# Image 0 of the symmetric attention with eight transposed runs instead of seven, and the schedule marks moved with them

## The chip, the cores and the metric

The kernel runs on one core of one Trainium2 chip. The metric is the device time of one launch in microseconds; three launches of the kernel before gave 2438.45, 2439.52 and 2439.89 us, and the profiled execution is a fourth one with a time of its own.

The core has five engines with a queue each: TensorE (PE in the profile; PEld is the loading of its weights), VectorE (DVE), ScalarE (ACT), GpSimd (POOL), and SyncE (SP), which here only issues transfers.

## The reference

Four layers run over four images of 64 x 64 pixels and 64 channels, in fp32:

```python
x = _L0_conv_ref(x, ...)   # attention over 4096 pixels: out = softmax(q k^T)^T v ; gamma*out + x
x = _L1_conv_ref(x, ...)   # layer norm, 64->256, 3x3 depthwise, gate, ->64 ; layer norm, MLP
x = _L2_conv_ref(x)        # attention of x with itself, see below
x = _L3_conv_ref(x, ...)   # attention over 4096 pixels with 32 channels, then batch norm
```

The change is in the third of these. It views the array as 64 rows of 4096 numbers per image, so that the scores are taken between entries of the second axis:

```python
B, C, H, W = x.shape
xf = x.reshape(B, C, H * W)
scores = jnp.einsum('bci,bcj->bij', xf, xf)
attn = jax.nn.softmax(scores, axis=-1)
out = jnp.einsum('bcj,bij->bci', xf, attn).reshape(B, C, H, W)
return out + x
```

`scores` is a 4096 x 4096 matrix for each image and it is symmetric: entry (i, j) equals entry (j, i). Its exponentials are therefore symmetric as well (a fixed shift is subtracted in place of the row's maximum), and only the division by the row's sum breaks the symmetry; the kernel divides at the end. The kernel uses this: a block of exponentials can serve twice, once as it is and once transposed.

## The kernel before, in words

The images go through the layers one after another, and two layers are always at work together. An image's layer 1 (vector work: stencils and norms) is cut into small pieces by Python generators and laid in between the pieces of the attention that runs at the time. Around the change it is image 0's symmetric attention (`layer2(0)`) that runs on TensorE, and layer 1 of image 3 (`layer1(3)`) that is laid in between. After it come the symmetric attention of image 1 and then layer 3 of image 0.

**Blocks and steps.** `layer2` cuts the 4096 x 4096 matrix into 8 x 8 blocks of 512 x 512. A pair (h, g) names the output columns h and the summed columns g. One block takes two *steps* (u = 0, 1). A step does this:

- `score`: four matmuls on the four 64 x 64 quarters of the array give a 128 x 1024 tile of scores in PSUM (line 1391; the profile shows eight records, since each fp32 matmul has two);
- two exponentials on ACT write it to an `e` tile in SBUF and leave row sums in `m.zs` (line 1396);
- `products`: four matmuls, again eight records, accumulate `x` times the `e` tile into the output of h (line 1453). They are issued two or three steps behind the scores.

**Transposed runs.** Block (g, h) is the transpose of block (h, g). In the list `PART` (image 0) or `FULL` (images 1 to 3) an integer g is a block used only as it is, and a pair in brackets is a *run*: two blocks, four steps, which are also used transposed, so that blocks (g, h) need not be computed at all. For each step of a run DVE transposes the `e` tile in 32 x 32 pieces into one of two `turned` tiles (line 1409). Three steps after the run's last one, `turned_products` issues 64 matmuls (128 records, line 1479) that read the run's `turned` tile and four rotated copies of `x` in the tile `xr`, and DVE adds the result into the output tile `A` (lines 1492 and 1494). Two of PSUM's three score slots are taken until that addition.

**Column sums.** A transposed block also needs its sums over the other axis. For image 0's group h = 0 POOL adds up the `e` tiles of the runs' steps (line 1432). For the groups h > 0 POOL instead issues one accumulating transfer of 512 KB for each step (line 1426), alternately into the two halves of an `esum` tile; a transfer waits until the one before it into the same half has landed. One more transfer adds the halves (line 1430), and POOL adds two quarters (line 1434). `spread_sums` later reduces the result on DVE (lines 1442 and 1443); it is issued nine steps after the group's last run step.

**Buffers.** The `e` tiles come from six buffers; two steps share one. `xr`, the `esum` tiles and the `own` tiles (copies of PSUM results, line 1465) take from the same six.

**Order.** The queues of PE, ACT, DVE and POOL hold their instructions in the order in which the Python code emits them. SP's queue is ordered by the compiler. The main loop calls item after item; every step of `layer2(0)` is an item, and each one advances two clocks, `conv` (layer 1 of image 3) and `misc`. A generator's piece is emitted when its clock has reached the time that its last `yield` named. In `layer2(0)` a step moves `conv` by 3.3, and by 1.5 in the seven steps around the end of one run, which `slow` names. In `layer2(1)` an item moves it by 3.2. `misc` moves by 1.8 a step and carries `features2(1)`, which transposes image 1's `x` into the keys `ko` (lines 1310, 1313, and transfers at line 1314); it is started at item `f + 88` of the 100 steps, f being the first.

**Layer 1 of image 3 beside it.** By the steps of `layer2(0)` in the kernel before: the first norm is at steps 3 to 12, the stencils (line 1241) run until about step 76, the second pointwise stage (line 1270) is at steps 80 to 83, the second norm (lines 1165 to 1192) from step 84 on, and the last pointwise stages (lines 1206, 1291, 1295) begin at step 99 and reach into image 1's symmetric attention.

Of the kernel before, what the change touches and what calls it, by code (L numbers as in the profile page):

```python
# [691 lines left out]
def fast_path(ctx: ExitStack, tc: tile.TileContext, a: dict, out: bass.AP, bad):  # L692
# [43 lines left out]
    def piece():  # L736
        if turn_of["banks"]:
            return PS[:, bass.ts(new_bank(), 512)]
        return new_ps()[:, 0:512]
# [14 lines left out]
    def new_big(name):  # L754
        return big.tile([128, 4096], F32, tag="big", name=name)
# [236 lines left out]
    def at(i, fn):  # L992
        due.setdefault(i, []).append(fn)
# [309 lines left out]
    def features2(b):  # L1303
        x = X[:, b]
        im[b].ko = ko = new_big("ko")
        kv = ko[:, 0:N].rearrange("p (a e n) -> p a e n", e=2, n=128)
        for g in range(4):
            ps = piece()
            for i in range(4):
                nc.tensor.transpose(ps[:, bass.ts(i, 128)], x[:, bass.ts(4 * g + i, 128)], ident)  # L1310
            for e, copy in enumerate((nc.vector.tensor_copy, nc.scalar.copy)):
                own, other = slice(64 * e, 64 * e + 64), slice(64 - 64 * e, 128 - 64 * e)
                copy(kv[own, bass.ts(g, 4), e, :], ps[own, :].rearrange("p (a n) -> p a n", n=128))
                nc.sync.dma_start(out=kv[other, bass.ts(g, 4), e, :], in_=kv[own, bass.ts(g, 4), e, :])
            yield 3.7
# [1 line left out]
    SIDES = [[(7, (h + 1) % 7), ((h + 2) % 7, (h + 3) % 7)] for h in range(7)]  # L1317
    FULL = [(7, [7])] + [(h, [h] + SIDES[h]) for h in range(6)] + [(6, SIDES[6] + [6])]
    PART = [
        (0, [0, 7, (1, 2), 5, (3, 4), 6]), (1, [1, 2, (5, 6), 3, 4, 7]), (2, [2, 1, 3, 4, 7]),  # L1320
        (3, [3, 1, 2, 4, 7]), (4, [4, 1, 2, 3, 7]), (7, [7, 0, 1, 2, 3, 4]),
        (6, [6, (2, 3), 0, (4, 7), 5]), (5, [5, (2, 3), (4, 7), 0, 6]),
    ]

    def layer2(b, when_free=None):
# [5 lines left out]
        steps, runs = [], []  # L1331
# [12 lines left out]
        begin = [mine[h][0] for h in range(8)]  # L1344
        spread_at = {mine_t[h][-1] + (5 if b else 9): h for h in m.mirrored}
        late_start = 4 if b else 6
        slow = range(runs[2][2] - 3, runs[2][2] + 4)
        used, todo, seen = {}, [], set()
        st = {"e": {}, "T": {}, "esum": {}}

# [185 lines left out]
    def close2(b):  # L1536
        x, m = X[:, b], im[b]
        ps, tot, n = piece(), sums2[:, b, :], 4 * max(m.mirrored) + 4
        cs = m.cs.rearrange("p (j k) -> p j k", k=4)
        for k in range(4):  # L1540
            mm(ps[32 * k : 32 * k + 32, 0:n], sel4, cs[:, 0:n, k], start=True, stop=True)
        g = 0
        while g < 8:
            k = g
            while k < 8 and m.count[k] == m.count[g]:
                k += 1
            nc.vector.tensor_reduce(
                tot[:, 4 * g : 4 * k],
                m.zs[:, m.first[g] : m.first[g] + 4 * m.count[g] * (k - g)]
                .rearrange("p (t k) -> p t k", k=m.count[g]), AX.X, ALU.add,  # L1550
            )
            g = k
        nc.vector.tensor_add(tot[:, 0:n], ps[:, 0:n], tot[:, 0:n])
        rz = sm.tile([128, 32], F32, tag="rz2", name="rz2")
        nc.vector.reciprocal(rz, tot)
        yield
        for i in range(4):
            ps = new_ps()
            for j in range(8):
                c = 1024 * i + 128 * j  # L1560
                nc.tensor.transpose(ps[:, bass.ts(j, 128)], m.A[:, c : c + 128], ident)  # L1561
            blocks_ = ps.rearrange("p (j n) -> p j n", n=128)
            nc.vector.tensor_mul(
                blocks_, blocks_, rz[:, bass.ts(i, 8)].unsqueeze(2).to_broadcast([128, 8, 128])
            )
            xs = x[:, bass.ts(i, 512)].rearrange("p (j h) -> p j h", h=H)
            for o in range(2):
                nc.vector.tensor_add(xs, ps.rearrange("p (j o h) -> p j o h", j=8, o=2)[:, :, o, :], xs)  # L1568
            yield
# [9 lines left out]
    def open3(b):  # L1579
        x, m = X[:, b], im[b]  # L1580
        m.tg = new_big("tg")
        m.th = m.tg[:, 0:1024]
        m.gx = m.tg[:, 1024:2048].rearrange("p (t d) -> p t d", d=32)
        for nb in range(2):
            ps = piece()
            for jj in range(2):
                for s in range(2):
                    k = 2 * s + jj
                    mm(
                        ps[32 * k : 32 * k + 32, :], thw[64 * s : 64 * s + 64, :],  # L1590
                        tok(x, s, 2 * nb + jj), start=True, stop=True,
                    )
            nc.vector.tensor_scalar_add(m.th[:, bass.ts(nb, 512)], ps, V("L3_conv_theta_b"))
            yield 3.0

        m.own = own = m.tg[:, 2048:3072].rearrange("p (s n) -> p s n", s=2)
        for s in range(2):
            ps = piece()
            for j in range(4):
                mm(  # L1600
                    ps[32 * j : 32 * j + 32, :], phw[64 * s : 64 * s + 64, :],
                    tok(x, s, j), start=True, stop=True,
                )
            nc.vector.tensor_scalar_add(own[:, s, :], ps, V("L3_conv_phi_b"))
            yield 3.0
        for i in range(2):
            ps = piece()
            for t in range(8):
                mm(ps[:, bass.ts(t, 64)], x[:, bass.ts(8 * i + t, 128)], gw, start=True, stop=True)
            for s in range(2):  # L1610
                nc.vector.tensor_add(
                    m.gx[:, 16 * s + 8 * i : 16 * s + 8 * i + 8, :],
                    ps.rearrange("p (t s d) -> p t s d", s=2, d=32)[:, :, s, :],
                    gb.unsqueeze(1).to_broadcast([128, 8, 32]),
                )
            yield 3.0

    def keys3(b):
        m = im[b]
        m.ph = new_big("ph")  # L1620
        keys = m.ph.rearrange("p (s n) -> p s n", s=2)
        for j in range(4):
            for k in range(4):
                nc.sync.dma_start(
                    out=keys[32 * k : 32 * k + 32, :, bass.ts(j, 512)],
                    in_=m.own[32 * j : 32 * j + 32, :, :],
                )
# [185 lines left out]
    conv_from, misc_from, misc_to = {}, {}, {}  # L1813
# [9 lines left out]
    for b in range(B):  # L1823
        misc_to[len(items)] = True
        f = len(items)
        if b == 0:
            layer2(b)
            misc_from[f + 88] = [features2(b + 1)]
        else:
            layer2(b, lambda b=b: keys3(b - 1))  # L1830
            turns = close2(b - 1)
            for i in (9 if b == 1 else 8, 11, 21, 31, 41):
                at(f + i, lambda turns=turns: next(turns))
            misc_from[f + 46] = [open3(b - 1)]
            f = len(items)
            misc_to[f] = True
            layer3(b - 1)
            if b + 1 < B:
                turns = features2(b + 1)
                for i in (4, 7, 10, 13):  # L1840
                    between3[f + i] = 2, lambda turns=turns: next(turns)
    f = len(items)
# [174 lines left out]
@with_exitstack  # L2017
def conv_seq_kernel(ctx: ExitStack, tc: tile.TileContext, a: dict, out: bass.AP):
    nc = tc.nc
    flag = ctx.enter_context(tc.tile_pool(name="flag", bufs=1))  # L2020
    bad = flag.tile([1, 1], mybir.dt.int32, name="bad")
    fast_path(tc, a, out, bad)
    n_bad = nc.values_load(bad[0:1, 0:1], min_val=0, max_val=1 << 20)
    with tc.If(n_bad > 0):
        general_path(tc, a, out)
# [37 lines left out]
```

## Time and profile before

| | us |
|---|---|
| median of three launches | 2439.52 (2438.45 to 2439.89) |
| the profiled execution, its own time | 2438.81 |
| its span, first to last instruction | 2437.0 |
| first score of image 0's symmetric attention | 1014.57 |
| first score of image 1's symmetric attention | 1246.44 |
| start of score steps 10, 16, 62, 74 and 86 of image 0 | 1041.00, 1058.88, 1149.93, 1171.03, 1200.58 |

So the part that changes, `layer2(0)`, takes 231.87 us of the span. All times below are counted from the span's start. In a line of groups the columns are: line, engine and operation, tiles and shapes, how many, then busy time, the mean duration of one in ns, and the engine's idle time ahead of them with what ended it. A line of the timeline has its start, the length of the merged piece, engine, line and operation, tiles, and how many instructions are merged; matmuls overlap, so a piece's length is longer than the distance to the next.

### The profile page before, as it was taken

What the parts mean: (1) busy time and instruction counts of PE and PEld (TensorE: products, weight loads), DVE (VectorE), ACT (ScalarE), POOL (GpSimd) and SP (SyncE); (2) the same over time, 40 slices, a digit from 0 to 9 for tenths busy, and PEclk for the clock granted to TensorE, in tenths of its full rate; (3) what the DMA queues carried; (4) which work ended last, traced back from release to release, by engine and by line L of the source; (5) the groups of instructions that cost most, each with busy time, mean ns of one, the idle gap of its engine ahead of it and who ended that gap; (6) DMA issues with size and microseconds to landing.
All of it is one profiled execution on the core that took longest, in us unless ns stands there. A gap on an engine that the chain in (4) does not pass through costs nothing.

```text
span 2437.0 us, 63657 instructions
## 1 busy us (share of the span) xinstructions
PE 2408.3 (99%) x27509; PEld 914.1 (38%) x27509; DVE 1461.6 (60%) x1787; ACT 1643.0 (67%) x3140; POOL 553.5 (23%) x395
## 2 busy tenths in 40 slices
PE   9999999999999999999999999999999999999998
PEld 3343453336433543343344442144421344421113
DVE  2020278227832774278667668876668766678886
ACT  4656766666666666668655459954479744579996
POOL 2000000000000000030136562256632365622220
PEclk9999999999999999999999999999999999999999
DMA  3000000010000000030540028710076400386665
GB/s 80 1 18 1 19 1 19 18 19 1 19 18 6 14 19 18 20 77 2 113 97 20 20 65 155 156 28 23 16 153 136 96 21 21 76 169 140 136 136 134
DMA packets 68390, 139.03 MB, mean 57 GB/s; under 512 B 13084, under 2 KB 34309, under 8 KB 68101
## 3 DMA queue, kind: packets, MB, share of 16 engines
q0 software_dynamic: 25040, 89.17, 18.3%
q1 hardware_dynamic: 42309, 43.85, 8.0%
q8 instruction: 218, 3.57, 0.6%
q10 hardware_dynamic: 752, 1.85, 0.2%
q14 instruction: 71, 0.58, 0.1%
HBM read 4.80 MB, written 4.19 MB: 4 GB/s over the span
## 4 chain that ended last, share of the span: by engine, by line
PE 90%; DVE 4%; ACT 4%; issue 1%; DMA 0%; SPq 0%; ACTq 0%; DVEq 0%
PE PS L1096 18%; PE PS L1122 18%; PE PS L1391 10%; PE PS L1453 10%; PE PS L1646 9%; PE PS L1707 9%; PE PS L1479 7%; PE PS L1206 2%; ACT e L1657 2%; DVE tg L1698 1%; ACT e L1396 1%; PE PS L1171 1%; PE PS L1270 1%; PE PS L1561 1%; PE PS L1064 1%
## 5 line engine op out<-in xcount | busy, mean ns | idle before, releaser
L1101 ACT ACTIVATE e<-PS 128x1024 f32<-128x1024 f32 x512 | 523.7, 1023 | 337.7 <-PE PS L1096 301.7
L1396 ACT ACTIVATE e<-PS 128x512 f32<-128x512 f32 x632 | 370.9, 595 | 329.7 <-PE PS L1391 310.5
L1096 PE MATMUL PS<-X,q 64*64 64x512 f32 x4096 | 573.6, 590 | 2.6 <-DVE X L979 1.7
L1122 PE MATMUL PS<-e,vq 64*64 64x512 f32 x4096 | 575.8, 592 | 0.0
L1657 ACT ACTIVATE e<-PS 128x512 f32<-128x512 f32 (+2 forms) x588 | 500.1, 920 | 58.3 <-PE PS L1646 37.5
L1698 DVE TENSOR_TENSOR tg<-tg,e 128x2048 f32<-128x2048 f32 x165 | 377.8, 2290 | 51.1 <-ACT e L1657 40.9
L1391 PE MATMUL PS<-ko 64*64 64x512 f32 x2528 | 334.3, 596 | 0.9 <-DVE X L1568 0.5
L1453 PE MATMUL PS<-e,X 64*64 64x512 f32 x2528 | 327.3, 590 | 1.1 <-ACT own L1465 1.1
L1432 POOL TENSOR_TENSOR esum<-esum,e 128x1024 f32<-128x1024 f32 x132 | 314.0, 2379 | 60.2 <-ACT e L1396 52.9
L1241 DVE SCALAR_TENSOR_TENSOR y<-pad,vec,y 128x1024 f32<-128x1024 f32 x240 | 308.9, 1287 | 18.2 <-ACT y L1237 10.9
L1432 POOL TENSOR_TENSOR esum<-e 128x1024 f32<-128x1024 f32 x22 | 52.2, 2371 | 1177.2 <-ACT e L1396 1171.4
L1409 DVE STREAM_TRANSPOSE turned<-e 128x1024 f32<-128x1024 f32 x196 | 240.6, 1238 | 108.5 <-ACT e L1396 108.2
L1646 PE MATMUL PS<-tg,ph 32*64 32x512 f32 x4096 | 294.9, 612 | 1.7 <-ACT e L1657 0.8
L1096 PEld LDWEIGHTS PS<-X,q 64*64 64x64 f32 x4096 | 182.9, 133 | 262.3 <-issue 181.5
L1122 PEld LDWEIGHTS PS<-e,vq 64*64 64x64 f32 x4096 | 183.5, 133 | 253.3 <-issue 156.3
L1707 PE MATMUL PS<-e,tg 128*32 128x512 f32 x2048 | 272.5, 604 | 0.0
L1679 POOL DMA_DIRECT2D xn<-e x130 | 113.3, 898 | 319.5 <-ACT e L1657 225.9
L1109 DVE TENSOR_REDUCE sums<-zs 128x1 f32<-128x4 f32 x128 | 19.7, 154 | 275.0 <-ACT e L1101 274.8
L1453 PEld LDWEIGHTS PS<-e,X 64*64 64x64 f32 x2528 | 97.5, 133 | 174.1 <-issue 154.4
L1391 PEld LDWEIGHTS PS<-ko 64*64 64x64 f32 x2528 | 90.0, 132 | 167.8 <-issue 145.5
L1646 PEld LDWEIGHTS PS<-tg,ph 32*64 32x64 f32 x4096 | 63.3, 129 | 222.7 <-ACT e L1657 190.2
L1396 ACT ACTIVATION_READ_ACCUMULATOR e<-PS 128x1 f32 x632 | 127.2, 201 | 0.0
(219 smaller groups left out, 1681.2 us busy)
## 6 DMA issues: line engine op xcount, KB each, us to landing
xn<-e POOLq DMA_DIRECT2D x146, 512.0 KB, 5.3
esum<-e POOLq DMA_DIRECT2D x20, 512.0 KB, 5.4
xn<-t SPq DMA_DIRECT2D x64, 128.0 KB
ph<-tg SPq DMA_DIRECT2D x64, 128.0 KB
xn<-X SPq DMA_DIRECT2D x224, 32.0 KB
xr<-X SPq DMA_DIRECT2D x176, 32.0 KB
ko<-ko SPq DMA_DIRECT2D x32, 128.0 KB
xr<-in_x_dram SPq DMA_DIRECT2D x13, 256.0 KB
```

What stands on the lines that cost most here:

```text
L1096: mm(ps[64 * c : 64 * c + 64, bass.ts(r, 512)], m.q[rows_, 128 * t + 64 * c : 128 * t + 64 * c + 64], x[rows_, bass.ts(g, 512)], start=Tru ...
L1101: act(es[g // 2][:, bass.ts(g % 2, 1024)], ps, AF.Exp, bias=SHIFT0, accum_out=zs[:, g : g + 1],)
L1122: ins = mm(PS[64 * s : 64 * s + 64, 2048 + 512 * j : 2560 + 512 * j], vq[rows_, :], es[j // 2][rows_, k : k + 512], start=t == 0 and i < 2 ...
L1241: stt(y1, win, wt, y1, ALU.mult, ALU.add)
L1391: mm(ps[64 * c : 64 * c + 64, bass.ts(r, 512)], m.ko[rows_, k : k + 64], m.ko[rows_, bass.ts(h, 512)], start=True, stop=True,)
L1396: act(e[:, bass.ts(r, 512)], ps[:, bass.ts(r, 512)], AF.Exp, bias=SHIFT2, accum_out=slot(g, 2 * u + r),)
L1432: nc.gpsimd.tensor_add(esum, st["e"][mine_t[h][0]] if k == 1 else esum, e)
L1453: mm(st["acc"][r][64 * c : 64 * c + 64, :], xw[rows_, 4 * g + 2 * u + c, :], st["e"][n][rows_, bass.ts(c, 512)], start=n == mine[h][0], st ...
L1646: mm(PS[64 * c : 64 * c + 64, bass.ts(banks[k], 512)], m.ph[32 * k : 32 * k + 32, 128 * mc + 64 * c : 128 * mc + 64 * c + 64], m.th[32 * k ...
L1657: act(e[:, 512 * lo : 512 * k], PS[:, 512 * banks[lo] : 512 * banks[lo] + 512 * (k - lo)], AF.Exp,)
L1698: nc.vector.tensor_add(esum, esum, e)
L1707: mm(st["y"][32 * k : 32 * k + 32, :], m.gx[:, i % 32, :], es[i][:, bass.ts(k, 512)], start=mc == 0, stop=i % 32 == 31,)
```

## The change

Two rows of `PART` are reordered and shortened, and one row is shortened.

- Group h = 0 had the order 0, 7, run (1, 2), 5, run (3, 4), 6. It becomes 0, 5, run (1, 2), run (3, 4), run (6, 7): blocks 6 and 7, computed directly before, are now also used transposed. Its steps 4 to 15 are all run steps.
- Group 7 no longer computes block 0 and group 6 no longer computes block 0, since these are the transposes of the new run. Group 6 becomes 6, 5, run (2, 3), run (4, 7).

In all 96 steps instead of 100, and eight runs instead of seven. The new run takes index 2, so `slow` names run 3 for image 0 (the same run (1, (5, 6)), still ending at step 23), and `features2(1)` starts at item `f + 84`, which is again twelve items before the end.

```diff
     PART = [
-        (0, [0, 7, (1, 2), 5, (3, 4), 6]), (1, [1, 2, (5, 6), 3, 4, 7]), (2, [2, 1, 3, 4, 7]),
-        (3, [3, 1, 2, 4, 7]), (4, [4, 1, 2, 3, 7]), (7, [7, 0, 1, 2, 3, 4]),
-        (6, [6, (2, 3), 0, (4, 7), 5]), (5, [5, (2, 3), (4, 7), 0, 6]),
+        (0, [0, 5, (1, 2), (3, 4), (6, 7)]), (1, [1, 2, (5, 6), 3, 4, 7]), (2, [2, 1, 3, 4, 7]),
+        (3, [3, 1, 2, 4, 7]), (4, [4, 1, 2, 3, 7]), (7, [7, 1, 2, 3, 4]),
+        (6, [6, 5, (2, 3), (4, 7)]), (5, [5, (2, 3), (4, 7), 0, 6]),
     ]
...
-        slow = range(runs[2][2] - 3, runs[2][2] + 4)
+        slow = range(runs[3 if b == 0 else 2][2] - 3, runs[3 if b == 0 else 2][2] + 4)
...
         if b == 0:
             layer2(b)
-            misc_from[f + 88] = [features2(b + 1)]
+            misc_from[f + 84] = [features2(b + 1)]
```

## The prediction, made before the result was known

> **What bounds the kernel now.** I read the page's busy shares and chain first, then its part around image 0 by stretches of time, then TensorE's own timeline there.
>
> ```profile
> PE 2408.3 (99%) x27509; PEld 914.1 (38%) x27509; DVE 1461.6 (60%) x1787; ACT 1643.0 (67%) x3140; POOL 553.5 (23%) x395
> ...
> PE 90%; DVE 4%; ACT 4%; issue 1%; DMA 0%; SPq 0%; ACTq 0%; DVEq 0%
> ```
>
> ```profile
> 1014.50:1043.00 28.50, 27.43 (x240) 8.68 (x240) 10.17 (x14) 17.63 (x49) 7.09 (x3) 1.00 0.33 68
> 1043.00:1070.00 27.00, 26.88 (x440) 12.51 (x437) 18.24 (x20) 18.52 (x49) 11.05 (x5) 1.00 0.05 12
> 1070.00:1171.00 101.00, 99.91 (x1024) 36.54 (x1020) 90.91 (x94) 82.35 (x235) 5.73 (x7) 1.00 0.15 35
> 1171.00:1210.00 39.00, 39.00 (x518) 15.18 (x514) 21.41 (x32) 23.32 (x67) 8.52 (x10) 1.00 0.70 150
> 1210.00:1246.40 36.40, 34.92 (x492) 15.59 (x488) 19.63 (x26) 20.87 (x59) 6.41 (x8) 1.00 0.85 175
> ```
>
> The five lines of the second fence are stretches: length, then busy us of PE, PEld, DVE, ACT, POOL, the granted clock, the DMA share, GB/s. PE is busy nearly throughout, at full clock. DVE is nearly full only while the stencils run (90.91 of 101); before 1070 it idles 27 of 55.5 us. Transfers matter only at the end (0.70 and 0.85). "Busy" alone does not show that PE issues without pauses, so I read distances between starts:
>
> ```profile
> 1058.02 1.04 PE L1453 MATMUL PS<-e,X 64*64 64x512 f32 x8
> 1058.88 1.04 PE L1391 MATMUL PS<-ko 64*64 64x512 f32 x8
> 1059.74 1.04 PE L1453 MATMUL PS<-e,X 64*64 64x512 f32 x8
> 1060.71 3.71 PE L1479 MATMUL PS<-turned,xr 32*64 32x256 f32 x128
> 1064.35 1.09 PE L1391 MATMUL PS<-ko 64*64 64x512 f32 x8
> 1065.26 1.04 PE L1453 MATMUL PS<-e,X 64*64 64x512 f32 x8
> ```
>
> A score group and a product group each follow the last after 0.86 us, however long they look, and most of the 231.87 us has this cadence. Adding up every pause over it between 1010 and 1246 gives only 4.5 us. So this part is bound by the number of matmul groups, and what the change takes away there should show.
>
> [...] here a run starts 0.97 after the group ahead of it and the second group after it lies 0.91 from the first, 0.16 more than the cadence. [...] a 512 KB accumulating transfer takes about 5.5 us at 1184 and 9.3 us (1218.08 to 1227.35) while SP's transfers are under way.
>
> **Removed from PE.** Blocks (7, 0) and (6, 0): 2 blocks x 2 steps x (score + product) = 8 groups x 0.86 = 6.88 us. ACT loses 4 x 2 exponentials with their sum readings, 8 x (0.60 + 0.20) = 6.4 us, off the path.
>
> **Added to PE.** One transposed run. Ahead, 1059.74 to 1065.26 is 5.52 us; without the run these would be two groups, 1.72. So 3.80 us. Net on PE: 6.88 - 3.80 = 3.08, **-3.1 us**.
>
> **Added elsewhere.** DVE: 4 transposes x 1.24 + 4 additions to `A` x 0.415 = 6.6, and 0.69 more in group 7, whose block 7 is no longer fresh in `A`. The 6.6 fall into steps 8 to 19, where DVE idles 27 us; there they cost nothing. Without that cover, among the stencils, DVE has 10 us idle in 101: it would still find room, with the stencils up to 6.6 us later and PE waiting for their pieces by at most that. The third run's product is issued at item 18, three steps after its transposes. POOL: four more additions x 2.37 = 9.5 us, eleven in a row from 1032; with the two later runs PE needs about 33 us for these steps, POOL 26, so it is never far behind. The `turned` tile of run 2 is that of run 0, read at item 10 and rewritten from item 12: no wait.
>
> **SP.** The rotated copies for h = 6 wait for the last turned product of h = 0. That moves from 1064.4 to about 1071, so they are issued at 1071 to 1082 in place of 1064 to 1075, and those for h = 5 shift likewise from 1085. They are needed at about 1188; the next thing behind them on SP begins at 1175 today. Free.
>
> **Layer 1 of image 3.** Steps 0 to 95 move its clock as before, so its pieces stay at the same step numbers. Four lost steps x 3.3 = 13.2 ticks go to image 1's part, 13.2 / 3.2 = 4 items later. Its PE work is the same and PE bounds that part too (52.76 of 53.6 busy, pauses of 1 us). Zero, either way 1 us.
>
> **The end of the part, where steps and side work meet anew.** Steps 74 and on are the same run, 3.8 us later (1174.8). But group 6's second run now follows the first without a break, group 5 starts at 82, its run at 84, and the keys `ko` come at items 84 to 90 instead of 88 to 94, so that the second norm (84 to 88) falls among them. Three things could run late.
>
> ```profile
> 1196.91 0.86 POOL L1426 DMA_DIRECT2D esum<-e  x1 [1.98 <-ACT e L1396]
> 1202.87 0.86 POOL L1430 DMA_DIRECT2D esum<-esum  x1 [5.09 <-DMA esum<-e]
> 1207.97 1.27 POOL L1434 TENSOR_TENSOR esum<-esum 128x512 f32<-128x512 f32 x1 [4.24 <-DMA esum<-esum]
> ...
> 1215.39 0.65 PE L1310 MATMUL PS<-ident,X 128*128 128x128 f32 x4 [0.17 <-ACT ko L1313]
> ...
> 1220.30 0.65 PE L1310 MATMUL PS<-ident,X 128*128 128x128 f32 x4 [0.66 <-ACT ko L1313]
> ...
> 1225.20 0.66 PE L1310 MATMUL PS<-ident,X 128*128 128x128 f32 x4 [0.66 <-ACT ko L1313]
> ```
>
> First, `e` buffers. Eight transfers in two alternating chains from 1178, about 6 us per pair, end near 1202, the final one and POOL's addition near 1209. Only then can group 5's first two transfers go out; landing near 1216. At step 90 all six buffers are taken (`xr`, two `esum`, steps 84 to 89), so its exponential needs those two landed. PE gets there near 1221: 5 us to spare. Second, the pauses at the key transposes: PE waits for a copy on ACT, which waits for one on DVE behind a transpose. Beyond the usual 0.5 us between groups they make 0.25 + 0.74 + 0.74, and the run after them took 4.53 instead of 3.71: 2.5 us today. They may vanish or double, -2.5 to +2.5; the same neighbours recur, so I take 0. Third, the norm's matmuls waited 1.3 us for ACT among run steps at 1027 and wait for nothing at 1201; 0 to +1.3, I take 0.
>
> **Sum.** Against the profiled execution: span 2437.0 - 3.1 = 2433.9; with 1.8 around it, 2435.7 instead of 2438.81. The runs' median lies 0.7 above that execution, so 2439.52 - 3.1 = **2436.4 us**. 0.2% is 4.9 us, about what a measurement of this kernel can tell from no change; the gain is under it.
>
> **Rivals.**
> - *Less waiting as well.* The crowded end loosens: transfers start 4 us earlier and keys 1 and 2 leave before the norm's eight transfers. If the 2.5 us of pauses go, 2433.9. For: SP now sends six of eight key transfers after the norm's. Against: the ACT-behind-DVE chain does not depend on transfers.
> - *Keys late.* SP's order is the compiler's. The norm's eight transfers took 13 us (1214.0 to 1227.0) and six key transfers went behind them, until 1238, eight us before image 1's first score, which needs the last keys. The norm now starts near 1219 and that score comes near 1242; keys behind it would cost up to 3 us: 2439.4.
> - *Slower: the chain of accumulating transfers becomes the bound.* From 1178 to the release for step 90 there are six transfers in a row with 5 us to spare; each may take 0.8 us longer before PE waits. At the 9.3 us seen under load, 3.5 longer, 21 - 5 = 16 us lost: 2452. Against: group 6's chain ran beside 32 of SP's transfers at 5.1 to 6.1 us each, and in the new order has much the same company.
>
> **Chances and range.** As forecast 0.57, less waiting 0.22, keys late 0.12, chain 0.09. The likeliest case's own range is 2434.0 to 2439.0 (the norm, 1 us of layer 1, half of the key pauses). The range of all, 2432.5 to 2441.0, takes in -2.5 with 1 us more, and +2.5 + 1.3 with 0.8 more; it leaves out the chain and some 0.07 at the low end. Faster than 2434.6: 0.20 of the second case and 0.03 of the first, 0.23. Slower than 2444.4: the chain and 0.01 of late keys, 0.10. The rest, 0.67.
>
> **What would show it.** Right: 96 score steps, 8 x 128 records at line 1479; image 1's first score near 1242.5 to 1243.5, since one group of layer 1 also slips behind it; step 62 near 1153.7, 3.8 later than today; step 90 with no wait for POOL's transfers. Wrong: pauses over 1 us among steps 8 to 19 (DVE or POOL late), an exponential at step 90 or later that waits for `esum`, a first score of image 1 that waits for SP, or a difference that appears only after 1300.

## The result

Six launches of the changed kernel gave 2447.46 to 2450.97 us, median 2449.15; six of the kernel before on the same chip 2438.45 to 2439.89, median 2439.14. The ratio is 1.0041, interval 1.0031 to 1.0052: slower by 10.0 us, where 2436.4 was forecast and 2441.0 was the upper end. The profiled execution took 2450.52 us, its span is 2448.7.

The page of the changed kernel first, its busy times and the shares of the chain that ended last:

```profile
PE 2410.6 (98%) x27573; PEld 916.8 (37%) x27573; DVE 1468.4 (60%) x1796; ACT 1639.5 (67%) x3123; POOL 565.5 (23%) x399
...
PE 44%; DVE 6%; ACT 3%; issue 1%; DMA 0%; SPq 0%; ACTq 0%; DVEq 0%; POOL 0%
```

PE has 64 more matmul records, as the change implies (128 for the new run, less 64 for the eight groups that went), and its busy time rose by only 2.3 us. In the chain POOL is new, with 0%, and the shares add up to 54% where they were 99%: followed back from the end, the chain breaks off in the middle of the span. Its earliest pieces in order of time (start, length) are these:

```profile
1095.40 0.15 POOL cs L1440
...
1095.58 0.04 DVE cs L1443
...
1097.80 0.34 DVE A L1492
...
1098.18 1.99 PE PS L1391 x8
```

It ends at a POOL instruction of 0.2 us that waited for no other engine's work. Stretches of image 0's part, in the columns of the kernel before, show the same place:

```profile
1014.90:1043.00 28.10, 27.02 (x232) 8.43 (x224) 12.51 (x16) 17.39 (x49) 10.11 (x5) 1.00 0.32 69
1043.00:1070.00 27.00, 27.00 (x516) 14.60 (x520) 18.85 (x19) 17.58 (x46) 19.71 (x8) 1.00 0.01 3
1070.00:1108.00 38.00, 31.22 (x382) 11.85 (x366) 26.05 (x31) 16.72 (x52) 5.16 (x7) 0.91 0.41 98
```

The third is unlike the others: PE idles 6.8 of 38 us and the clock is 0.91. TensorE's timeline there (start, length, then in brackets the idle time ahead and what ended it):

```profile
1090.22 1.09 PE L1391 MATMUL PS<-ko 64*64 64x512 f32 x8
1091.13 1.04 PE L1453 MATMUL PS<-e,X 64*64 64x512 f32 x8
1098.18 1.99 PE L1391 MATMUL PS<-ko 64*64 64x512 f32 x8 [6.01 <-DVE A L1492]
1099.94 1.93 PE L1453 MATMUL PS<-e,X 64*64 64x512 f32 x8
1101.65 1.93 PE L1391 MATMUL PS<-ko 64*64 64x512 f32 x8
1103.36 1.40 PE L1453 MATMUL PS<-e,X 64*64 64x512 f32 x8
1104.59 1.03 PE L1391 MATMUL PS<-ko 64*64 64x512 f32 x8
```

Step 28's score starts 7.05 us after the group ahead of it instead of 0.86, which is 6.19 lost. The next four groups take 6.41 us (1098.18 to 1104.59) instead of 4 x 0.86 = 3.44: 2.97 more. Together 9.16 us. PE waits for DVE's additions to `A`, which free the score slots of run 3. So VectorE's timeline:

```profile
1085.12 0.70 DVE L1442 STREAM_TRANSPOSE esum<-esum 128x512 f32<-128x512 f32 x1
1095.58 0.69 DVE L1443 TENSOR_REDUCE cs<-esum 128x16 f32<-128x512 f32 x1 [9.76 <-POOL cs L1440]
...
1097.38 0.42 DVE L1494 COPY A<-PS 128x256 f32<-128x256 f32 x1
```

DVE wasn't busy. It stood for 9.76 us at `spread_sums` of group 0, whose reduction waits for POOL's line 1440, and run 3's additions (its matmuls ended at 1090.3) stood behind it. Line 1440 is `nc.gpsimd.memset(m.cs, 0.0)`: the zeroing of the tile that receives all column sums of the image, 0.20 us long, issued inside `spread_sums` when that is called for image 0's first group. POOL's timeline shows why it was late:

```profile
1077.15 0.57 POOL L1426 DMA_DIRECT2D esum<-e  x1 [8.99 <-ACT e L1396]
...
1083.12 0.87 POOL L1426 DMA_DIRECT2D esum<-e  x1 [0.83 <-ACT y L1237]
1089.24 0.86 POOL L1430 DMA_DIRECT2D esum<-esum  x1 [5.25 <-issue]
1094.15 1.26 POOL L1434 TENSOR_TENSOR esum<-esum 128x512 f32<-128x512 f32 x1 [4.04 <-DMA esum<-esum]
1095.35 0.20 POOL L1440 MEMSET cs<- 128x128 f32 x1
```

Line 1426 issues the four accumulating transfers of group 1's run, at steps 20 to 23; the first and the last of them are shown. The next (line 1430) adds the two halves and waits until the last of the four has landed (the line names no releaser, but the trace has that landing at 1088.73, just ahead of 1089.24); the addition waits until that one has landed in turn. The zeroing, which waits for nothing of its own, is queued behind both and starts at 1095.35, as the addition ends (1095.41). The kernel before, same view:

```profile
1076.15 0.90 POOL L1426 DMA_DIRECT2D esum<-e  x1 [1.68 <-DMA esum<-e]
1076.72 0.55 POOL L1440 MEMSET cs<- 128x128 f32 x1
1078.01 0.87 POOL L1426 DMA_DIRECT2D esum<-e  x1 [0.74 <-DMA esum<-e]
```

There it lay between the third and the fourth transfer, and DVE reached its reduction at 1078.90 without a wait. The group's last run step was 13 and is now 15, so the call of `spread_sums`, nine steps behind it, went from item 22 to item 24, while group 1's run stayed at steps 20 to 23: the call, and POOL's instruction in it, was moved past the last two transfers.

That is most of it, not all. I cut the two traces at the first scores of images 0, 1 and 2 and sorted TensorE's time by what each group computes (distance from one start to the next). "Image 1's part" runs from image 1's first score to image 2's; layer 3 of image 0 lies in it.

| distance of starts, after minus before, us | image 0's part | image 1's part |
|---|---|---|
| scores | -2.89 | 0.00 |
| products | +5.69 | +3.31 |
| transposed runs | +4.27 | +0.63 |
| last stages of layer 1 (L1206, L1295) | -0.91 | +0.3 |
| norms of layer 1 (L1171) | -0.18 | |
| all | +5.99 | +4.24 |

The 9.16 us are in image 0's column. But image 1's part, which the change doesn't touch, lost 4.2 us too; of these 0.9 are a group of line 1206 that now falls behind the cut.

### The profile page after: what moved, and what is told of

Its sections match the earlier page's. It is cut to its first block, busy times and chain, and to the rows that moved or that the text cites. A ratio compares the mean times of both kernels' runs of the same rounds, so it can differ in the third digit from the quotient of the medians.

```text
span 2448.7 us, 63782 instructions
## 1 busy us (share of the span) xinstructions
PE 2410.6 (98%) x27573; PEld 916.8 (37%) x27573; DVE 1468.4 (60%) x1796; ACT 1639.5 (67%) x3123; POOL 565.5 (23%) x399
## 4 chain that ended last, share of the span: by engine, by line
PE 44%; DVE 6%; ACT 3%; issue 1%; DMA 0%; SPq 0%; ACTq 0%; DVEq 0%; POOL 0%
PE PS L1646 9%; PE PS L1707 9%; PE PS L1391 8%; PE PS L1453 8%; PE PS L1479 7%; ACT e L1657 2%; DVE y L1241 2%; DVE tg L1698 1%; ACT e L1396 1%; DVE turned L1409 1%; PE PS L1609 1%; PE PS L1561 1%; DVE A L1468 0%; PE PS L1600 0%; PE PS L1206 0%
## 5 line engine op out<-in xcount | busy, mean ns | idle before, releaser
L1432 POOL TENSOR_TENSOR esum<-esum,e 128x1024 f32<-128x1024 f32 x136 | 324.8, 2388 | 62.3 <-ACT e L1396 54.7
```

Source lines behind the costliest of these rows:

```text
L1432: nc.gpsimd.tensor_add(esum, st["e"][mine_t[h][0]] if k == 1 else esum, e)
```

## The experiments

Two theories stand behind most of the expectations. **Theory M**: the zeroing's place in POOL's queue cost some 9 us. **Theory S**: the four lost steps shift the last pieces of layer 1 of image 3 by four items, and where they now lie in image 1's part they cost some 3 us. The rivals for the first are that the third run itself overloads DVE around steps 19 to 28, or that a later reduction costs in proportion to its lateness; for the second, that the loss comes from the new order at the end of image 0's part, the keys above all. Here are all the runs, with both parts from each profiled execution. The ratio is not the quotient of the two medians; the two differ most where the launches of one kernel scatter (e7, e8, e12).

| kernel | median, us | before beside it | ratio and interval | image 0's part | image 1's part |
|---|---|---|---|---|---|
| before | 2439.14 | | | 231.87 | 338.85 |
| after | 2449.15 | 2439.14 | 1.0041, 1.0031 to 1.0052 | 237.86 | 343.09 |
| e1_memset_first | 2440.32 | 2439.07 | 1.0004, 0.9995 to 1.0013 | 229.26 | 343.10 |
| e2_before_spread24 | 2447.24 | 2439.07 | 1.0032, 1.0020 to 1.0045 | 239.86 | 338.86 |
| e3_spread22 | 2440.79 | 2439.07 | 1.0006, 0.9997 to 1.0015 | 229.12 | 343.08 |
| e4_spread23 | 2449.85 | 2439.07 | 1.0043, 1.0026 to 1.0060 | 238.86 | 343.08 |
| e5_before_shift | 2442.28 | 2439.17 | 1.0013, 1.0006 to 1.0020 | 230.83 | 343.46 |
| e6_fix_spread_conv | 2441.58 | 2439.17 | 1.0011, 1.0004 to 1.0017 | 234.29 | 338.88 |
| e7_fix_keys83 | 2443.10 | 2439.17 | 1.0013, 1.0006 to 1.0020 | 231.41 | 343.40 |
| e8_keys82 | 2445.63 | 2439.17 | 1.0022, 1.0012 to 1.0032 | 239.02 | 339.84 |
| e9_fix_early_conv | 2441.75 | 2439.41 | 1.0010, 1.0002 to 1.0018 | 233.41 | 338.88 |
| e10_before_early_conv | 2442.07 | 2439.41 | 1.0012, 1.0005 to 1.0018 | 239.81 | 334.50 |
| e11_fix_early_conv2 | 2446.75 | 2439.41 | 1.0030, 1.0018 to 1.0041 | 239.04 | 338.90 |
| e12_fix_even_conv | 2439.91 | 2439.27 | 1.0008, 1.0000 to 1.0017 | 233.35 | 338.84 |

### The zeroing

**e1: the changed kernel, with the zeroing at step 0.** The allocation of its tile goes with it; nothing else moves.

```diff
+                if b == 0:
+                    m.cs = sm.tile([128, 128], F32, tag="cs2", name="cs2", bufs=1)
+                    nc.gpsimd.memset(m.cs, 0.0)
...
-            if h == m.mirrored[0]:
+            if h == m.mirrored[0] and b:
...
-                if b == 0:
-                    nc.gpsimd.memset(m.cs, 0.0)
```

> The changed kernel, with one edit: the zeroing of cs on POOL is emitted at step 0 of image 0 instead of with the first reduction of column sums at step 24. Theory M (the zeroing, moved in POOL's queue behind the four transfers of group 1, their final transfer and POOL's addition, held DVE for 9.8 us, so PE for 6.6 us and then at half clock): the 9.2 us that steps 27 to 32 took longer than before go away, 2449.2 - 9.2 = 2440.0 (2438.5 to 2441.5), and step 27 to step 28 takes 1.7 to 1.8 us. Theory D (DVE simply has too much to do with four more transposes and copies among the stencils): no change, 2448 to 2450. Theory C (the accumulating transfers of groups 6 and 5 bound the end of the part): no change either.

Measured: 2440.32 us, 8.8 below the changed kernel. The reduction is issued at the same place as after the change and no longer waits (its lines have numbers one to three higher in this kernel); run 3's additions follow as soon as the run lets them:

```profile
1085.21 0.70 DVE L1443 STREAM_TRANSPOSE esum<-esum 128x512 f32<-128x512 f32 x1
1085.95 0.69 DVE L1444 TENSOR_REDUCE cs<-esum 128x16 f32<-128x512 f32 x1
...
1090.60 0.42 DVE L1495 COPY A<-PS 128x256 f32<-128x256 f32 x1 [2.78 <-PE PS L1480]
```

The work is the same, with one 0.2 us instruction elsewhere. Theory M holds and the rival of an overloaded DVE falls. Image 1's part is unchanged at 343.1.

**e2: the kernel before, with group 0's reduction at step 24**, that is, the mark's move alone, without the third run.

```diff
-        spread_at = {mine_t[h][-1] + (5 if b else 9): h for h in m.mirrored}
+        spread_at = {mine_t[h][-1] + (5 if b else 11 if h == 0 else 9): h for h in m.mirrored}
```

> The kernel before, with one edit: the first reduction of column sums (group 0), and the zeroing of cs with it, at step 24 instead of 22; all blocks and runs as before. Theory M: in POOL's queue the zeroing now comes after the addition that ended at 1090.7, DVE waits for it from about 1081, and the copies of run 2, which PE needs for step 28, come some 6 us late; with slow clock after it 6 to 9 us are lost: 2445 to 2448.5. Theories D and C: nothing was added to DVE and nothing changed at the end: 2439.1 within 1.

Measured: 8.2 us slower than before, with the same signature in POOL's, DVE's and PE's timelines:

```profile
1090.51 0.20 POOL L1440 MEMSET cs<- 128x128 f32 x1
```

```profile
1090.74 0.69 DVE L1443 TENSOR_REDUCE cs<-esum 128x16 f32<-128x512 f32 x1 [9.86 <-POOL cs L1440]
```

```profile
1093.34 1.98 PE L1391 MATMUL PS<-ko 64*64 64x512 f32 x8 [6.32 <-DVE A L1494]
```

So the loss needs no third run. Image 1's part is as before to 0.01 us: the 4.2 us there have another cause.

**e3 and e4: the changed kernel, with the reduction at step 22 and at step 23.** If what counts is the number of steps, e4 should lie between e3 and the changed kernel; if it is the place between two transfers, e3 recovers all and e4 nothing.

```diff
-        spread_at = {mine_t[h][-1] + (5 if b else 9): h for h in m.mirrored}
+        spread_at = {mine_t[h][-1] + (5 if b else 7 if h == 0 else 9): h for h in m.mirrored}
```

(e4 has 8 in place of 7.)

> The changed kernel, with the reduction of group 0 and its zeroing at step 22, two steps earlier, where the kernel before had it. Theory M: the zeroing goes out between POOL's transfers of group 1, as before: 2440.0 (2438.5 to 2441.5). Theories D and C: 2448 to 2450.

> The changed kernel, with the reduction of group 0 and its zeroing at step 23, one step earlier. Theory M, by the place in POOL's queue: step 23 is the last of group 1's run, whose last transfer, final transfer and addition are emitted ahead of the reduction in the same step, so the zeroing is as late as at step 24: 2447.5 to 2450.5. If the loss came from the reduction being late in time, in proportion to the steps, this would lie half way, near 2444.5.

Measured: 2440.79 for e3, the same as e1; in it the zeroing goes out at 1081.34 between transfers three and four. e4 took 2449.85, as slow as the changed kernel. There the zeroing comes at 1095.56, and since DVE reaches the reduction a step sooner, it waits a step longer, 10.77 us instead of 9.76. It is a threshold between two neighbours of one queue and not a slope.

### Image 1's part

**e5: the kernel before, with layer 1's clock standing still in the last four steps.** Image 3's pieces reach image 1's part 13.2 ticks behind, as after the change; the rest is the kernel before.

```diff
-                conv.tick(1.5 if n in slow else 3.3)
+                conv.tick(0.0 if n >= 96 else 1.5 if n in slow else 3.3)
```

> The kernel before, with one edit: the last four of the 100 steps of image 0 do not move the clock of layer 1 of image 3, so that its last pieces meet image 1's part four items later, as in the changed kernel; nothing else changes. Theory S (with the zeroing out of the way 3.4 us of the forecast gain are lost because these pieces now meet the closing of image 0 and the transposes of image 1, where PE waits for DVE): 2439.1 + 1.5 to 3.5, so 2440.5 to 2442.5. Rival (the loss has to do with the runs and the keys at the end of image 0, not with these pieces): 2439.1 within 0.7.

Measured: 2442.28, 3.1 us slower, and image 1's part 343.46. The chain of waits settles it. TensorE's waits in image 1's part (what waits, for whom: total us, times, longest), first the changed kernel, then this run, then the kernel before:

```profile
PE PS L1479 <- DVE X L1568: 1.3, 1, 1.3
PE PS L1479 <- DVE u L1291: 0.6, 1, 0.6
PE PS L1206 <- DVE X L1568: 0.5, 1, 0.5
PE PS L1391 <- DMA ko<-ko: 0.3, 1, 0.3
PE PS L1453 <- DVE A L1468: 0.3, 1, 0.3
```

```profile
PE PS L1479 <- DVE X L1568: 1.3, 1, 1.3
PE PS L1479 <- DVE u L1291: 0.6, 1, 0.6
PE PS L1206 <- DVE X L1568: 0.5, 1, 0.5
PE PS L1206 <- ACT e L1396: 0.3, 1, 0.3
PE PS L1453 <- DVE A L1468: 0.3, 1, 0.3
```

```profile
PE PS L1391 <- DVE X L1568: 0.5, 1, 0.5
PE PS L1391 <- DVE u L1291: 0.4, 1, 0.4
```

Four of the waits are the same ones to 0.1 us. Only the wait for the keys' transfers is the changed kernel's own. It is 0.3 us here and 1.2 us in e1, and since it ends with image 1's first score it belongs to image 0's part. Theory S holds, and the keys explain nothing of the 4.2 us in image 1's part.

**e7 and e8: the keys sooner.** e7 is e1 with `features2(1)` one item earlier; e8 is two items earlier, together with the faster clock of e6 below.

```diff
-            misc_from[f + 84] = [features2(b + 1)]
+            misc_from[f + 83] = [features2(b + 1)]
```

> The changed kernel with the zeroing at step 0, and with the keys of image 1 started one item earlier (83). With the zeroing moved, the first score of image 1 waited 1.2 us for the last keys, which SP sent behind the second norm's transfers. If the last two key transfers stay behind the norm's, nothing changes (2440.3); if they come ahead of some of them, the wait goes and 2439.1 is reached.

> Both edits of the run before last (zeroing at step 0, 3.96 in the last 20 steps), and the keys of image 1 started two items earlier (82). If theory S and the wait for the keys add up, 2435.5 to 2437.5, under the kernel before by its 3.1 us or nearly; if the keys' copies at items 82 to 88 hold PE at the denser pieces, as much as the run without this edit or more.

Measured: both slower, 2443.10 and 2445.63, against 2440.32 of e1 and 2441.58 of e6. In e7 the 1.2 us for the keys' transfers are gone, as hoped. But a transposed run waits 1.8 us for the key copy on ACT, and a group of line 1206 waits 1.4 us for the norm on DVE. In e8 a transposed run waits 2.3 us for ACT, and a group of line 1206 waits 2.8 us for DVE's additions at 1246.5. After that last wait the clock stood at 0.50 to 0.51 for 6.00 us (last section). So the wait for the keys can be removed, but starting them earlier cost more than the 1.2 us it gave back.

### Can the shift be undone?

e6, e9, e11 and e12 start from e1 and let layer 1 run faster in image 0's part, so that it reaches image 1's part where it did before: in the last 20 steps, in steps 6 to 19, in steps 8 to 15, and evenly. e10 has e9's edit in the kernel before, as a control. "The first of these three", in the text for e11, is e9.

```diff
-                conv.tick(1.5 if n in slow else 3.3)
+                conv.tick(1.5 if n in slow else 3.96 if n >= 76 else 3.3)           # e6
+                conv.tick(1.5 if n in slow else 4.25 if 6 <= n < 20 else 3.3)       # e9, e10
+                conv.tick(1.5 if n in slow else 4.95 if 8 <= n < 16 else 3.3)       # e11
+                conv.tick(1.5 if n in slow else 3.45)                               # e12
```

> The changed kernel with the zeroing at step 0, and with the clock of layer 1 of image 3 moved by 3.96 instead of 3.3 in each of the last 20 steps of image 0 (13.2 in all, what the four lost steps took away). Theory S: its last pieces meet image 1's part where they did before, most of the 3.4 us come back, 2436.5 to 2438.5. Rival: still 2440.3, or worse where the denser pieces at the end of image 0 hold PE.

> The changed kernel with the zeroing at step 0, and with the clock of layer 1 of image 3 moved by 4.25 instead of 3.3 in steps 6 to 19 of image 0 (13.3 in all, what the four lost steps took away), where DVE idled half of the time. From step 20 on, layer 1 then stands four steps further, so that its second norm and its last pieces meet the end of image 0 and image 1's part as in the kernel before. Theory P (the run itself gains the 3.1 us of the sum, and the rest was lost to the changed company): 2436.0 to 2437.5. Rival (the second run of group 6 right behind the first costs what the sum gains, whatever the company): 2438.5 to 2440.5.

> The kernel before with the same edit of the clock in steps 6 to 19 and nothing else: a control. If the earlier layer 1 is worth something by itself, this is faster than 2439.1 too, by as much as it explains of the run above. Theory P: the pieces at the end now come four steps early and leave image 1's part sooner, so 2437.5 to 2440; no gain of 3 us by itself.

> As the first of these three, with the 13.2 ticks put into steps 8 to 15 alone (4.95 a step). Theory P: the same 2436.0 to 2437.5, unless the first pieces of the stencils now hold PE; then up to 1.5 us more. Rival: 2438.5 to 2440.5.

> The changed kernel with the zeroing of the sums' tile early, and layer 1 of image 3 moved by 3.45 instead of 3.3 in every step outside the slow ones: 89 x 0.15 = 13.35 ticks, which is what the four lost steps took (13.2). The catch-up is spread evenly, where it was put into the first steps or the last ones in the runs before this one and lost there what it won in image 1. Theory S, that the pieces of layer 1 which slip into image 1's part cost about 3 us there and that an even catch-up costs nothing in image 0's part: 2440.3 - 3.1 = 2437.2 us, 2436.0 to 2438.4, with image 1's part back at about 339 us and image 0's part at most 230. Rival, that layer 1 has no slack anywhere in image 0's part: 2440 to 2443, with image 1's part at about 339 us but image 0's part at 231 or more.

Measured: wherever the catch-up was put, image 1's part came back to 338.84 to 338.90, 4.2 us shorter than in e1, and image 0's part grew by nearly the same: 5.0 us in e6, 4.15 in e9, 4.1 in e12. The control e10 shows the same exchange from the other side: 4.35 us won in image 1's part, 7.9 lost in image 0's. e11, with the same catch-up in only eight steps, lost some 6 us against e1. So the times forecast by theories S and P were missed in all five runs; e9 and e11 came out slower than their rival's range as well, and e6 and e12 lie at or near theirs. In e6 and e11 the clock fell in stretches of image 0's part, to a mean of 0.63 over 2.70 us from 1207.30 and to 0.50 over 3.00 us from 1072.30, which makes their losses larger; in e10 the four groups after a wait, from 1070.05 to 1075.23, took 5.18 us instead of 3.44. In e9 the clock was 1.00 around a wait of 2.4 us (1063.00 to 1070.00), and e12's mean over its profiled execution was 0.999. No version beat the kernel before; e12's 2439.91 is 0.64 above it, interval 1.0000 to 1.0017. VectorE and TensorE of e12, at the run that ends at 1046.5, show one such loss:

```profile
1043.42 1.25 DVE L1412 STREAM_TRANSPOSE turned<-e 128x1024 f32<-128x1024 f32 x1 [1.33 <-ACT e L1399]
1044.59 4.48 DVE L1192 TENSOR_TENSOR xn<-xn,X 128x1024 f32<-128x1024 f32 x2
1048.99 1.40 DVE L1495 COPY A<-PS 128x256 f32<-128x256 f32 x4
```

```profile
1046.50 1.09 PE L1394 MATMUL PS<-ko 64*64 64x512 f32 x8
1049.78 1.09 PE L1206 MATMUL PS<-xn,pw 64*64 64x512 f32 x8 [2.20 <-DVE A L1495]
```

DVE idles 1.33 us, then two norm operations of 2.24 us each stand in front of the run's additions, and PE waits for those. On average DVE has room in this stretch; in the order of its queue it hasn't, since every run brings a moment at which PE needs it at once. Later in the same kernel another 2.1 us are lost to such an addition, at 1077.7; the two waits together are 4.3 us, and image 0's part grew by 4.1. The third run isn't needed for such a loss: in e10, which doesn't have it, an addition held PE for 3.2 us at 1070.05.

## Why the prediction was wrong, point by point

- **"Removed from PE" and "Added to PE", net -3.1: right for the matmul groups.** In e1, where the zeroing is out of the way, image 0's part is 2.61 us shorter, of which 0.91 is a group of layer 1 that slipped into image 1's part, as the prediction said. So 1.7 of the 3.1 arrived; new waits, below, took the rest. Scores and products fell by 5.81 (6.88 less some new pauses), transposed runs rose by 4.27: 3.64 for one more run, from its start to the next group's, and 0.63 because slowed runs lost more than before. (The other 0.16 of the forecast 3.80 lies in the groups around the run.)
- **The step that failed: what the change moves.** The prediction went through PE, DVE, POOL and SP for the third run, and through the marks `slow` and `features2`. It didn't look at the third mark that follows the run list, `spread_at`. The description of the kernel gives its rule ("nine steps after the group's last run step") but only the two DVE lines of `spread_sums`, not the zeroing on POOL. With the mark went one POOL instruction past two transfers. "POOL ... is never far behind" counted the additions of group 0, and these indeed ended at 1068.2, before group 1's first transfer at 1077.15. What held POOL was not work but a wait for landings, from 1083.1 on. Measured: +8.8 us by medians (e1), 9.16 by the trace. None of the signs that the prediction lists looks at steps 24 to 28, where it happened.
- **"Layer 1 of image 3. Zero, either way 1 us": wrong.** The argument was that PE bounds image 1's part too, and that the work is the same. Both are true and didn't matter; it is the neighbours that differ. Measured by itself (e5): +3.1 us. The prediction priced three meetings of steps and side work at the end of image 0's part from single waits; this one it dismissed by an average.
- **"They cost nothing" for DVE's 6.6 us in steps 8 to 19: almost.** Steps 8 to 18 kept their cadence. At step 20 the score waited 0.8 us for the additions of run 2, which stood behind two stencils (2.59 us at 1071.09): step 20 is 4.60 us later than before against the start of the part in e1, where 3.80 was forecast. And line 1270 waits 0.7 us for DVE at 1197, which is new.
- **The end of the part: right on balance.** The pauses at the key transposes went, 1.5 us in the list of waits of before, none after; two runs were slowed (4.62 and 4.25 us long instead of 3.71), where before it was one (4.53), and the first score of image 1 waited 0.3 us for its keys, 1.2 in e1. So "less waiting" and "keys late" both happened, and nearly cancelled.
- **The rival "slower", by the chain of accumulating transfers: right sign, wrong place.** Group 6's and group 5's transfers waited for each other, but no exponential of these steps waited for `esum`. What decided was the first such chain, group 1's, near 1083, and through an instruction that has nothing to do with it.
- **The time.** Without the zeroing's loss the changed kernel is at 2440.3 (e1). That lies inside the range given, but by luck: the range was made wide mainly for other losses, at the end of the part. Against the kernel before beside it e1 is 1.25 us slower where 3.1 faster was forecast, so 4.3 us are missing. The shift of layer 1 explains 3.1 of them (e5). Most of the rest lies in image 0's part, which by the trace is 1.4 us longer than forecast. There e1's list of waits has three that are new, 1.2 us for the keys, 0.8 at step 20 and 0.7 at line 1270, and has lost the 1.5 at the key transposes.

Left open: the 0.8 us at step 20 and the 0.7 at line 1270 weren't tried alone, and the keys' 1.2 us were removed only together with a new loss (e7). Whether another rate in image 1's own items would take the shifted pieces without waits wasn't tried either; so what is shown is that the shift costs 3 us and that image 0's part can't absorb it at four rates, not that no schedule can.

## What to carry to other kernels

When an edit moves a call, list every instruction it issues on every engine and, for each, the instructions it is moved past: a 0.2 us memset behind two waits for landings cost 9 us, and sat in no busy time. Give instructions without inputs (a zeroing, an allocation) the earliest place, so that no queue's waits can stand in front of them (8.8 us in e1). And work that is laid in beside a saturated engine isn't free because its engine idles on average: moved by four items it met other neighbours and gave back as much as the shorter loop was to win (3.1 us in e5).

## What the runs showed of the hardware

TensorE's pause in the changed kernel, idle for 6.01 us, cost more than its length. The granted clock after it was 0.50; this is its view by stretches:

```profile
1092.00:1098.00 6.00, 0.17 (x4) 0.00 (x0) 2.42 (x4) 0.63 (x3) 1.40 (x2) 0.94 0.43 94
1098.00:1104.00 6.00, 5.82 (x28) 1.79 (x32) 5.86 (x8) 1.64 (x5) 0.00 (x0) 0.50 0.14 36
1104.00:1108.00 4.00, 4.00 (x40) 1.29 (x36) 2.68 (x3) 2.77 (x11) 0.00 (x0) 0.99 0.00 0
```

Four groups ran at 0.50 and cost 2.97 us beyond the pause. e8 shows the same after a much shorter pause, idle for 2.81 us:

```profile
1246.50:1249.50 3.00, 2.98 (x16) 1.05 (x20) 0.62 (x2) 0.93 (x1) 0.87 (x1) 0.50 0.18 37
1249.50:1252.50 3.00, 3.00 (x19) 0.75 (x15) 0.00 (x0) 0.18 (x1) 0.00 (x0) 0.51 0.80 150
```

In e9 the clock was 1.00 after a pause that ended at 1066.67, idle for 2.42 us:

```profile
1066.60:1070.00 3.40, 3.33 (x32) 1.28 (x36) 3.40 (x5) 1.74 (x5) 2.85 (x2) 1.00 0.01 2
```

But the length of the pause didn't decide it in these runs. In e6 a pause after the first four matmul records of a transposed run, idle for 1.87 us, was followed by stretches with means of 0.63 and 0.76:

```profile
1207.30 5.96 PE L1480 MATMUL PS<-turned,xr 32*64 32x256 f32 x124 [1.87 <-ACT e L1399]
```

```profile
1207.30:1210.00 2.70, 2.70 (x44) 1.78 (x52) 2.50 (x4) 0.66 (x3) 0.00 (x0) 0.63 0.85 165
1210.00:1213.00 3.00, 3.00 (x90) 2.28 (x74) 0.00 (x0) 0.45 (x1) 1.80 (x2) 0.76 0.51 102
```

In e12 TensorE was idle for 2.20 us (until 1049.78) and for 2.08 (until 1077.72), and each time the second group after the pause started 0.91 us behind the first; in the changed kernel at 0.50 that was 1.76 (1098.18 to 1099.94). In e2, after 6.32 us of idle, the clock was 0.51 over 3.00 us from 1093.30. Launches of one kernel differed too: ten of e12's took 2439.48 to 2440.19 us at a mean clock of 0.998 to 0.999, three took 2444.09 to 2446.84 at 0.996 to 0.997.

How long the clock stood at 0.50 follows from the stretches (a mean of 0.63 over 2.70 us is half clock for 2.0 of them): 3.4 us in e6, 6.8 in the changed kernel, 6.8 in e2 (0.71 over 6.80 us from 1086.50, then 0.51 over 3.00) and 10.2 in e4 (0.71 over 6.30 us from 1092.00, then 0.50 over 6.00 and 0.90 over 3.00). In e2 3.9 of the 6.8 fell into the pause, where they cost nothing, so it lost 1.5 us, and the changed kernel, where 0.9 did, lost 3.

Half clock followed 1.87 us of idle in e6 and didn't follow 2.42 in e9; what decides isn't shown by these runs. On top of the pause it cost 1.5 us in e2 and 3 in the changed kernel.
